# A message-passing layer on one core: two groups of edges in every stage of a step instead of one

## The chip, the core and the metric

The kernel runs on one core of one Trainium2 chip. A core has five engines with an instruction stream each: TensorE (PE: matrix products, with weight loads listed apart as PEld), VectorE (DVE), ScalarE (ACT), GpSimd (POOL) and SyncE (SP, which here only issues DMA transfers). They run side by side and wait for one another through semaphores. SBUF is the on-chip working memory, with 128 partitions; PSUM, to which PE writes, has eight banks of 512 fp32 values in each partition. The metric is the device time of one execution in microseconds (us), lower is better; the median of several runs is given.

## The reference

One graph layer with a residual and a layer norm, on N = 6250 nodes of D = 128 values and E = 100,000 edges sorted by destination, with a hidden width of H = 256. `layernorm` subtracts each row's mean and divides by the root of its variance plus 1e-5.

```python
msg_in = concatenate([x[src], x[dst]], axis=-1)          # E x 256
h = relu(msg_in @ Wm1 + bm1)                             # E x 256
h = relu(h @ Wm2 + bm2)                                  # E x 256
messages = h @ Wm3 + bm3                                 # E x 128
agg = segment_sum(messages, dst) / clip(count(dst), 1)   # N x 128
upd = relu(concatenate([x, agg]) @ Wn1 + bn1) @ Wn2 + bn2
out = layernorm(x + (x + upd))
```

## The kernel before

There are three stages.

**Tables (0 to about 84 us).** The first product is taken per node, not per edge: `atab` holds `x @ Wm1[:128]` in fp32 in DRAM, `btab` holds `x @ Wm1[128:]` as three bf16 terms. Index columns, destination windows and the products `x @ Wn1[:128]` (`x_part`, line 327, blocks of 512 nodes) are made beside them. Four blocks of `x_part` are kept for the edge loop: 9 and 12 for its first steps (`X_FIRST`), 10 and 11 for its end (`X_END`).

**Edge loop (about 84 to 1127 us).** It is written out, not a loop on the chip. The edges are cut into NG = 196 groups of GE = 512 (the last has two tiles of 128, the others four). A group passes through these stages:

- `fetch` (lines 431 and 437): POOL gathers the four tiles' rows of `atab` by source with four indirect DMAs; SP loads the rows of `btab` for each tile's window of 21 destinations with four DMAs. A ring of four `rows` buffers holds them. `destinations` (line 355), issued by ACT, brings the destination numbers of two groups at a time.
- `hot` (lines 452 and 455, DVE): two one-hot matrices of the destinations, `oht` for the first layer and `oh` for the sums.
- `first_layer`: PE turns the gathered rows (line 468) and adds the destinations' terms as products with `oht` (line 474), both in PE tiles of 64 rows, into `ph` (two PSUM banks); ACT applies bias and relu into `h1` (line 478).
- `second_layer`: PE multiplies by `w2` (line 487), two tiles into one bank at a time, in full 128x128 tiles; DVE writes `max(product, -b2)` into one of four buffers `h2` (line 489).
- `sums`: PE adds up the edges of each window, `oh.T @ h2` (line 495), in tiles of 32 columns, four windows side by side; ACT copies the bank (`part_of`, line 502).
- `add_up`: PE turns those sums (line 511, tiles of 64 rows), and DVE adds each window to the accumulator `acc` in SBUF at a place read from `tilei` (lines 516 and 519).

fp32 products of lines 487 and 495 appear as two records each in the trace.

The order of PE is the written one (`manual_schedule`) from the tables on. In each step i of the loop it is: sums of group g - 3, turning of group g - 4, first layer of group g = i - 2, second layer of group g - 1. So a whole step lies between the end of a group's second layer and its sums. DVE and ACT follow the written order up to step 6 (`turns.close()`); from there a scheduler orders them. The PSUM pools of the loop are `p1` (`ph`, one buffer of two banks), `p2` (`ph2`, two buffers of one bank), `pa` (`pg`, one bank) and `ptp` (`pt`, two banks). A last block under `manual_schedule` ends the loop with the three last groups and the blocks 10 and 11 of `x_part`.

**Nodes (about 1127 to 1202 us).** After a barrier (and a loop for windows that span too many nodes, empty here) the accumulated hidden sums are multiplied by `Wm3`, divided by the counts and taken through the node products and the layer norm.

Around the edge loop, `late_loads`, the filler of `dpad` and `double` (the table `x2tab`: twice x plus a bias, for the end) are spread over the steps.

Of the kernel before, what the change touches and what calls it, by code (L numbers as in the profile page):

```python
# [19 lines left out]
P = 128  # L20
# [7 lines left out]
def kernel(  # L28
# [109 lines left out]
    w1 = const.tile([P, 2, H], F32, name="w1")  # L138
# [12 lines left out]
    with tc.tile_pool(name="prep", bufs=1) as prep, tc.tile_pool(  # L151
# [3 lines left out]
    ) as pb:  # L155
        src_i = prep.tile([R, 2 * GE], I32, name="src_i", tag="src_i")
# [256 lines left out]
    with edge, tc.tile_pool(name="wk", bufs=2) as wk, tc.tile_pool(  # L413
        name="p1", bufs=1, space=PSUM
    ) as p1, tc.tile_pool(name="p2", bufs=2, space=PSUM) as p2, tc.tile_pool(
        name="pa", bufs=1, space=PSUM
    ) as pa, tc.tile_pool(name="pt", bufs=1, space=PSUM) as ptp:


        NH2 = 4  # L420
# [4 lines left out]
        def fetch(idx, nt, firsts):  # L425


            rows = ld.tile([P, (GT + 1) * H], F32, name="rows", bufs=4)
            ag = rows[:, :GT * H].rearrange("p (j h) -> p j h", j=GT)
            for j in range(GT):  # L430
                nc.gpsimd.indirect_dma_start(  # L431
                    out=ag[:, j, :], out_offset=None, in_=atab[:, :],
                    in_offset=bass.IndirectOffsetOnAxis(ap=idx[:, j:j + 1], axis=0))
            bw = rows[:, GT * H:].bitcast(BF16).rearrange("p (k h) -> p k h", k=2)
            for j, first in enumerate(firsts):
                terms = btab[ds(first, WB + 1)].rearrange("n c h -> (n c) h")
                nc.sync.dma_start(bw[j // 2 * NQ:(j // 2 + 1) * NQ, j % 2, :], terms[:NQ])
            return ag, bw
# [7 lines left out]
        def hot(db, pb_cols, dl, nt):  # L446


            n = nt * WN
            oht = wk.tile([P, 2, P], BF16, name="oht")  # L450
            for k in range(2):
                nc.vector.tensor_scalar(oht[:n, k, :], db[:n, k * P:(k + 1) * P], pb_cols[:n, k:k + 1], None,  # L452
                                        op0=ALU.is_equal)
            oh = wk.tile([P, GT, WN], F32, name="oh", bufs=4)
            nc.vector.tensor_tensor(oh[:, :nt, :], iota_n.to_broadcast([P, nt, WN]),  # L455
                                    dl.rearrange("p (j o) -> p j o", o=1).to_broadcast([P, nt, WN]),
                                    op=ALU.is_equal)
            return oht, oh
# [3 lines left out]
        def first_layer(ag, bw, oht, nt):  # L462
            nh = nt // 2
            ph = p1.tile([P, 2, HC, 2 * P], F32, name="ph")
            for c in range(HC):
                for u in range(GT):
                    for h in range(nh):
                        nc.tensor.matmul(ph[:, h, c, u * NQ:(u + 1) * NQ], ag[halves[h], u, c * P:(c + 1) * P],  # L468
                                         ident[halves[h], halves[h]], is_transpose=True,
                                         start=(c == 0 and u == 0), stop=False, skip_group_check=True)  # L470
            for c in range(HC):
                for k in range(2):
                    for h in range(nh):
                        nc.tensor.matmul(ph[:, h, c, k * P:(k + 1) * P], bw[halves[h], k, c * P:(c + 1) * P],  # L474
                                         oht[halves[h], k, :], start=False, stop=True, skip_group_check=True)
            h1 = wk.tile([P, HC, GE], F32, name="h1")
            for c in range(HC):
                nc.scalar.activation(h1[:, c, :nh * 2 * P].rearrange("p (h e) -> p h e", h=nh), ph[:, :nh, c, :],  # L478
                                     AF.Relu, bias=b1[:, c:c + 1])
            return h1  # L480

        def second_layer(h1, h2, nt):
            for j0 in range(0, nt, 2):
                ph2 = p2.tile([P, 2, H], F32, name="ph2")
                for a in range(2):
                    for c in range(HC):
                        nc.tensor.matmul(ph2[:, a, :], h1[:, c, (j0 + a) * P:(j0 + a + 1) * P],  # L487
                                         w2[:, c, :], start=(c == 0), stop=(c == HC - 1))
                nc.vector.tensor_tensor(h2[:, j0:j0 + 2, :H], ph2, nb2.to_broadcast([P, 2, H]), op=ALU.max)  # L489

        def sums(oh, h2, nt):

            pg = pa.tile([P, H + 1], F32, name="pg")
            for j in range(nt):
                nc.tensor.matmul(pg[j * WN:(j + 1) * WN, :], oh[:, j, :], h2[:, j, :],  # L495
                                 start=True, stop=True, skip_group_check=True)
            return pg

        def part_of(pg, nt):
            n = nt * WN  # L500
            part = wk.tile([P, H + 1], F32, name="part")
            nc.scalar.copy(part[:n, :], pg[:n, :])  # L502
            return part

        def add_up(part, firsts, nt):
            pt = ptp.tile([P, 2, 4 * P], F32, name="pt")[:, :, :(HC + 1) * NQ]
            pt = pt.rearrange("p h (c q) -> p h c q", q=NQ)
            for c in range(HC + 1):
                for h in range(nt // 2):
                    rows = part[halves[h], c * P:(c + 1) * P] if c < HC else part[halves[h], H:].to_broadcast([NQ, P])  # L510
                    nc.tensor.matmul(pt[:, h, c, :], rows, ident[halves[h], halves[h]], is_transpose=True,  # L511
                                     start=True, stop=True, skip_group_check=True)
            for j in reversed(range(nt)):
                window = acc[:, :, ds(firsts[j], WB)]
                k = j % 2 * WN
                nc.vector.tensor_add(window, window, pt[:, j // 2, :, k:k + WB])  # L516
# [28 lines left out]
        def bank_p1():  # L545
            return p1.tile([P, 2, HC, 2 * P], F32, name="ph")[:, 0]

        def bank_p2():
            return p2.tile([P, 2, H], F32, name="ph2")

        ahead, lag = 2, 3
        st, hots = {}, {}
        first = list(X_FIRST)
        for i in range(NG + ahead + 1):
            if i == 6:
                turns.close()
            if i == 16:
                late_loads()

                none = wk.tile([16, (NG * GE - E) // 16 + 1], I32, name="none", bufs=1)  # L560
                nc.vector.memset(none, NONE)
                nc.sync.dma_start(dpad[E - 16:].rearrange("(p e) -> p e", p=16), none)
                nc.sync.dma_start(dpad[:E].rearrange("(p e) -> p e", p=16), dst.rearrange("(p e) -> p e", p=16))
            for step, after in enumerate((20, 24, 27)):
                if i >= after and (i - after) % 8 == 0 and (i - after) // 8 < len(pieces):
                    double((i - after) // 8, step)
            if i < NG:
                nt = GT if i < NGF else LT
                firsts = load_bases(tilei[0:1, i * GT:(i + 1) * GT], nt, ENG.SP)
                if i == NGF:  # L570
                    dbs = last_destinations()
                elif i % 2 == 0:
                    dbs = early.pop(0) if early else destinations(i, min(2, NGF - i), dst_row)
                st[i] = dict(nt=nt, got=fetch(srcT[:, i, :], nt, firsts), db=dbs.pop(0))
            g = i - ahead
            if 0 <= g < NG:
                s = st[g]
                ag, bw = s.pop("got")

                def make_hot(g):  # L580
                    s = st[g]
                    hots[g], s["oh"] = hot(s.pop("db"), pbase[:, g, :], dloc[:, g, :s["nt"]], s["nt"])

                if g not in hots:
                    make_hot(g)
                oht = hots.pop(g)
            k = g - lag
            pg = sums(st[k]["oh"], st[k]["h2"], st[k]["nt"]) if 0 <= k < NG else None
            k = g - lag - 1
            if 0 <= k < NG:  # L590
                s = st.pop(k)
                if "firsts" not in s:
                    s["firsts"] = load_bases(tilei[0:1, k * GT:(k + 1) * GT], s["nt"], ENG.DVE)
                add_up(s["part"], s["firsts"], s["nt"])
            if 0 <= g < NG:
                s = st[g]
                s["h1"] = first_layer(ag, bw, oht, s["nt"])
            if pg is not None:
                st[g - lag]["part"] = part_of(pg, st[g - lag]["nt"])
# [220 lines left out]
```

## Time and profile before

| | |
|---|---|
| median of 3 runs | 1203.84 us (1203.38 to 1206.65) |
| the profiled execution | 1204.24 us, its span 1202.5 us |
| granted TensorE clock, mean | 0.996 |
| HBM | 160 GB/s over the span |

The window view gives the busy time of each engine in a stretch (us):

| stretch | PE | DVE | ACT | POOL | granted clock |
|---|---|---|---|---|---|
| 0 to 60 | 51.76 | 39.36 | 40.28 | 34.99 | 1.00 |
| 70 to 100 | 27.25 | 16.46 | 12.44 | 22.79 | 1.00 |
| 300 to 500 | 200.00 | 104.06 | 62.01 | 144.47 | 1.00 |
| 500 to 700 | 200.00 | 108.51 | 62.31 | 144.50 | 1.00 |
| 900 to 1100 | 200.00 | 109.57 | 62.30 | 142.38 | 1.00 |
| 1100 to 1130 | 27.27 | 13.74 | 8.26 | 0.20 | 0.97 |
| 1145 to 1202 | 49.29 | 45.85 | 34.42 | 9.09 | 0.95 |

How to read the lines that follow in the next section. In the page's groups, a line has the source line, the engine, the operation, what it writes and reads, the shape and the number of instructions; after the bar the busy time in us and the mean duration of one in ns; after the second bar the idle time of the engine just before them and what ended most of it. In a timeline, a line has the start in us from the span's start, the length, the engine and the merged group, with the idle time before it and its releaser in brackets. Ends of matmuls are modelled, and consecutive matmuls overlap, so the starts carry the information.

### The profile page before, as it was taken

What the parts mean: (1) busy time and instruction counts of PE and PEld (TensorE: products, weight loads), DVE (VectorE), ACT (ScalarE), POOL (GpSimd) and SP (SyncE); (2) the same over time, 40 slices, a digit from 0 to 9 for tenths busy, and PEclk for the clock granted to TensorE, in tenths of its full rate; (3) what the DMA queues carried; (4) which work ended last, traced back from release to release, by engine and by line L of the source; (5) the groups of instructions that cost most, each with busy time, mean ns of one, the idle gap of its engine ahead of it and who ended that gap; (6) DMA issues with size and microseconds to landing.
All of it is one profiled execution on the core that took longest, in us unless ns stands there. A gap on an engine that the chain in (4) does not pass through costs nothing. (4 is left out here: it accounts for less than half of the span.)

```text
span 1202.5 us, 32806 instructions
## 1 busy us (share of the span) xinstructions
PE 1180.1 (98%) x11196; PEld 896.9 (75%) x11197; DVE 675.7 (56%) x2077; ACT 419.2 (35%) x776; POOL 801.2 (67%) x862
## 2 busy tenths in 40 slices
PE   8999999999999999999999999999999999999997
PEld 6747777777777777777777777777777777777565
DVE  5764555555555455555555555555555555555587
ACT  5753332332332333233233323323323332332256
POOL 6567777777777777777777777777777777773120
PEclk9999999999999999999999999999999999999998
DMA  8886666676555555555555555555555555552243
GB/s 274 280 264 191 183 194 185 182 193 185 160 151 153 150 148 153 152 151 152 152 149 147 153 153 152 153 150 149 148 154 154 150 152 151 147 147 67 83 117 114
DMA packets 173733, 193.66 MB, mean 161 GB/s; under 512 B 30906, under 2 KB 145548, under 8 KB 173548
## 3 DMA queue, kind: packets, MB, share of 16 engines
q0 software_dynamic: 38160, 103.75, 31.5%
q1 hardware_dynamic: 106956, 61.93, 17.7%
q10 hardware_dynamic: 28448, 25.87, 7.3%
q8 instruction: 89, 1.46, 0.5%
q14 instruction: 80, 0.66, 0.2%
HBM read 168.92 MB, written 22.88 MB: 160 GB/s over the span
## 5 line engine op out<-in xcount | busy, mean ns | idle before, releaser
L431 POOL DMA_INDIRECT rows<-atab,srcT x784 | 749.0, 955 | 285.4 <-issue 181.0
L487 PE MATMUL ph<-w,h 128*128 128x256 f32 x3128 | 727.6, 386 | 0.1
L487 PEld LDWEIGHTS ph<-w,h 128*128 128x128 f32 x3128 | 579.0, 190 | 91.1 <-ACT x_sb L329 0.9
L489 DVE TENSOR_TENSOR h<-ph,nb 128x512 f32<-128x512 f32 x391 | 270.6, 693 | 388.7 <-PE ph L487 376.4
L478 ACT ACTIVATE h<-ph,b 128x512 f32<-128x512 f32 x392 | 247.3, 682 | 138.4 <-PE ph L474 133.1
L502 ACT COPY part<-pg 128x257 f32<-128x257 f32 x196 | 73.6, 376 | 575.5 <-PE pg L495 510.6
L516 DVE TENSOR_TENSOR acc<-acc,pt 128x63 f32 x782 | 172.0, 220 | 78.1 <-PE pt L511 20.5
L468 PE MATMUL ph<-ident,rows 64*128 64x64 f32 x3128 | 129.9, 223 | 1.3 <-ACT h L478 0.7
L495 PE MATMUL pg<-h,oh 128*32 128x257 f32 x1564 | 125.6, 392 | 0.0
L468 PEld LDWEIGHTS ph<-ident,rows 64*128 64x128 f32 x3128 | 113.1, 140 | 2.3 <-ACT h L478 0.9
L511 PEld LDWEIGHTS pt<-ident,part 64*128 64x128 f32 x1173 | 51.1, 137 | 81.5 <-issue 81.1
L452 DVE TENSOR_SCALAR oht<-db,pbase 128x128 bf16<-128x128 int32 x392 | 100.9, 289 | 0.1
L495 PEld LDWEIGHTS pg<-h,oh 128*32 128x32 f32 x1564 | 30.9, 108 | 65.8 <-issue 65.0
L511 PE MATMUL pt<-ident,part 64*128 64x64 f32 x1173 | 77.8, 239 | 0.1
L474 PE MATMUL ph<-oht,rows 64*128 64x128 bf16 x1564 | 76.1, 216 | 0.9 <-DMA rows<-btab 0.8
L701 POOL TENSOR_TENSOR agg<-total,rc 128x512 f32<-128x512 f32 (+2 forms) x15 | 16.0, 1069 | 69.5 <-DMA rcol<-acc 33.2
L455 DVE TENSOR_TENSOR oh<-iota_n,dloc 128x128 f32<-128x128 f32 x196 | 55.9, 285 | 0.0
L474 PEld LDWEIGHTS <-rows 64*128 64x128 bf16 x1564 | 53.2, 96 | 1.4 <-DMA rows<-btab 0.9
L235 PE MATMUL pbt<-w,xT 128*128 128x256 f32 x196 | 49.8, 398 | 3.9 <-DVE rest L255 1.2
L235 PEld LDWEIGHTS pbt<-w,xT 128*128 128x128 f32 x196 | 36.6, 198 | 13.4 <-DVE rest L255 2.9
L724 PEld LDWEIGHTS pot<-wu,u 128*128 128x128 f32 (+1 forms) x196 | 24.0, 191 | 5.1 <-issue 4.5
L696 PE MATMUL pmt<-acc,w 128*128 128x512 f32 (+2 forms) x60 | 24.8, 551 | 2.3 <-DVE rc L690 2.3
(111 smaller groups left out, 410.7 us busy)
## 6 DMA issues: line engine op xcount, KB each, us to landing
rows<-btab SPq DMA_DIRECT2D x782, 32.0 KB
db<-in_dst_dram ACTq DMA_DIRECT2D x194, 128.0 KB
rows<-atab,srcT POOLq DMA_INDIRECT x784
btab<-bt SPq DMA_DIRECT2D x24, 384.0 KB
atab<-bt SPq DMA_DIRECT2D x24, 256.0 KB
xd<-in_x_dram SPq DMA_DIRECT2D x12, 256.0 KB
x2tab<-xd SPq DMA_DIRECT2D x12, 256.0 KB
x_sb<-in_x_dram SPq DMA_DIRECT2D x5, 512.0 KB
```

The costliest lines, as they stand in the source:

```text
L235: nc.tensor.matmul(pbt[:, a, :], xT[:, (t0 + a) * P:(t0 + a + 1) * P], w1[:, k, :], start=True, stop=True)
L431: nc.gpsimd.indirect_dma_start(out=ag[:, j, :], out_offset=None, in_=atab[:, :], in_offset=bass.IndirectOffsetOnAxis(ap=idx[:, j:j + 1], a ...
L452: nc.vector.tensor_scalar(oht[:n, k, :], db[:n, k * P:(k + 1) * P], pb_cols[:n, k:k + 1], None, op0=ALU.is_equal)
L468: nc.tensor.matmul(ph[:, h, c, u * NQ:(u + 1) * NQ], ag[halves[h], u, c * P:(c + 1) * P], ident[halves[h], halves[h]], is_transpose=True, ...
L474: nc.tensor.matmul(ph[:, h, c, k * P:(k + 1) * P], bw[halves[h], k, c * P:(c + 1) * P], oht[halves[h], k, :], start=False, stop=True, skip ...
L478: nc.scalar.activation(h1[:, c, :nh * 2 * P].rearrange("p (h e) -> p h e", h=nh), ph[:, :nh, c, :], AF.Relu, bias=b1[:, c:c + 1])
L487: nc.tensor.matmul(ph2[:, a, :], h1[:, c, (j0 + a) * P:(j0 + a + 1) * P], w2[:, c, :], start=(c == 0), stop=(c == HC - 1))
L489: nc.vector.tensor_tensor(h2[:, j0:j0 + 2, :H], ph2, nb2.to_broadcast([P, 2, H]), op=ALU.max)
L495: nc.tensor.matmul(pg[j * WN:(j + 1) * WN, :], oh[:, j, :], h2[:, j, :], start=True, stop=True, skip_group_check=True)
L502: nc.scalar.copy(part[:n, :], pg[:n, :])
L511: nc.tensor.matmul(pt[:, h, c, :], rows, ident[halves[h], halves[h]], is_transpose=True, start=True, stop=True, skip_group_check=True)
L516: nc.vector.tensor_add(window, window, pt[:, j // 2, :, k:k + WB])
```

## The change

The step of the loop now takes two groups (98 pairs, `NP`).

- `fetch`, `hot`, `first_layer`, `sums` and `part_of` get a list of groups. `rows` has two buffers of two groups, `ph` four banks (one buffer), `oht` and `h1` hold two groups; there are two `h2` buffers, one for each group of a pair, and six `oh`.
- The other four banks are the pool `p2`, two tiles of two banks (`banks()`), used in turn by `sums`, by the turning (`turned`, split off from `add_up`) and by the second layer of each group. `second_layer` writes a group's four products into one such tile; its max is one instruction (128x1024) for the first group of a pair and two of 128x512 for the second (`cuts`).
- A pair's step: sums of pair p - 2, turning of pair p - 3, then DVE's first addition, the copy of the sums, the other additions, the `x2tab` step, the comparisons for pair p + 1; PE's first layer of pair p; second layer of pair p - 1. The sums of a pair come directly after its second layer.
- The copy of the sums is one DVE instruction for both groups (128x514) instead of an ACT copy for each.
- DVE and ACT follow the written order to the end of the loop.
- `w1` moves to a pool that ends with the tables. The steps at which `late_loads` and `double` stand are halved. At the end, three products of `x_part` stand ahead of the last sums and one behind them.

```diff
-        def second_layer(h1, h2, nt):
-            for j0 in range(0, nt, 2):
-                ph2 = p2.tile([P, 2, H], F32, name="ph2")
-                for a in range(2):
-                    for c in range(HC):
-                        nc.tensor.matmul(ph2[:, a, :], h1[:, c, (j0 + a) * P:(j0 + a + 1) * P],
-                                         w2[:, c, :], start=(c == 0), stop=(c == HC - 1))
-                nc.vector.tensor_tensor(h2[:, j0:j0 + 2, :H], ph2, nb2.to_broadcast([P, 2, H]), op=ALU.max)
+        def banks():
+            return p2.tile([P, 2, 2 * H], F32, name="banks")
...
+        def second_layer(h1, h2, nt, cuts):
+            ph2 = banks().rearrange("p b (t h) -> p (b t) h", t=2)
+            for j in range(nt):
+                for c in range(HC):
+                    nc.tensor.matmul(ph2[:, j, :], h1[:, c, j * P:(j + 1) * P],
+                                     w2[:, c, :], start=(c == 0), stop=(c == HC - 1))
+            step = nt // cuts
+            for j in range(0, nt, step):
+                nc.vector.tensor_tensor(h2[:, j:j + step, :H], ph2[:, j:j + step],
+                                        nb2.to_broadcast([P, step, H]), op=ALU.max)
...
+        def sums(groups):
+            pg = banks()
+            for i, (oh, h2, nt) in enumerate(groups):
+                for j in range(nt):
+                    nc.tensor.matmul(pg[j * WN:(j + 1) * WN, i, :H + 1], oh[:, j, :], h2[:, j, :],
+                                     start=True, stop=True, skip_group_check=True)
+            return pg
...
-            nc.scalar.copy(part[:n, :], pg[:n, :])
+                nc.vector.tensor_copy(part[:, :n], pg[:, :n, :H + 1])
...
+        def turned(part, nts):
+            pt = banks()[:, :, :2 * (HC + 1) * NQ].rearrange("p h (g c q) -> p h g c q", g=2, q=NQ)
...
+        for i in range(NP + 4):
...
+            if i < NP:
+                dbs = early.pop(0) if early else destinations(2 * i, min(2, NGF - 2 * i), dst_row)
...
+                got = fetch([(srcT[:, 2 * i + k, :], firsts) for k, firsts in enumerate(bases(i, ENG.SP))])
...
+            p = i - 1
...
+            k = p - 3
+            firsts = bases(k, ENG.DVE) if k >= 0 else None
+            pg = pt = None
+            if 0 <= p - 2 < NP - 1:
+                pg = summed(p - 2)
+            if 0 <= k:
+                pt = turned(st[k]["part"], st[k]["nts"])
+            if p - 2 == NP - 1:
+                whole(x for x, _ in zip(rest, range(2)))
+                pg = summed(p - 2)
+                whole(rest)
+            adds = add_up(pt, firsts, st[k]["nts"]) if pt is not None else iter(())
+            next(adds, None)
+            if pg is not None:
+                st[p - 2]["part"] = part_of(pg, st[p - 2]["nts"])
+            whole(adds)
...
+            for step, after in enumerate((10, 12, 14)):
+                if i >= after and (i - after) % 4 == 0 and (i - after) // 4 < len(pieces):
+                    double((i - after) // 4, step)
+            if p + 1 < NP:
+                make_hot(p + 1)
+            if p < NP:
+                s = st[p]
+                s["h1"] = first_layer(s.pop("got"), s.pop("ohts"), s["nts"])
+            if p < 2:
+                whole(x_part(X_FIRST[p], bank, (nc.scalar, nc.vector)))
+            if 0 <= p - 1 < NP:
+                s = st[p - 1]
+                for k, nt in enumerate(s["nts"]):
+                    second_layer(s["h1"][:, k], h2s[k], nt, 1 + k)
```

`summed(p)` calls `sums` on both groups of pair p; `bases(p, engine)` reads the windows' first nodes of both groups into registers of that engine; `make_hot(p)` calls `hot` on both.

## Prediction, before the result was known

> **What bounds the kernel now.** I read the page first, then the timeline of one stretch of the edge loop, first TensorE alone, then all engines. The chain of waits is no help here: it reaches back only to the barrier before the node stage (5% of the span on PE).
>
> ```profile
> PE 1180.1 (98%) x11196; PEld 896.9 (75%) x11197; DVE 675.7 (56%) x2077; ACT 419.2 (35%) x776; POOL 801.2 (67%) x862
> ...
> PEclk9999999999999999999999999999999999999998
> ...
> L431 POOL DMA_INDIRECT rows<-atab,srcT x784 | 749.0, 955 | 285.4 <-issue 181.0
> L487 PE MATMUL ph<-w,h 128*128 128x256 f32 x3128 | 727.6, 386 | 0.1
> ```
>
> PE is busy 98% of the span at nearly the full granted clock, and its largest group idles 0.1 us in all. So TensorE's own stream is the bound, and what counts is how long one turn of it takes:
>
> ```profile
> 504.60 0.64 PE L495 MATMUL pg<-h,oh 128*32 128x257 f32 x8
> 505.17 0.40 PE L511 MATMUL pt<-ident,part 64*128 64x64 f32 x6
> 505.41 0.66 PE L468 MATMUL ph<-ident,rows 64*128 64x64 f32 x16
> 505.91 0.39 PE L474 MATMUL ph<-oht,rows 64*128 64x128 bf16 x8
> 506.22 3.72 PE L487 MATMUL ph<-w,h 128*128 128x256 f32 x16
> 509.87 0.64 PE L495 MATMUL pg<-h,oh 128*32 128x257 f32 x8
> ```
>
> Start to start a group costs 0.57 (sums) + 0.24 (turning) + 0.50 + 0.31 (first layer) + 3.65 (second layer) = 5.27 us, 10.55 a pair. The second number of a line is a modelled busy time that overlaps the next line; starts are what to add. The other engines around one such turn:
>
> ```profile
> 502.98 0.69 DVE L489 TENSOR_TENSOR h<-ph,nb 128x512 f32<-128x512 f32 x1 [0.95 <-PE ph L487]
> ...
> 504.59 0.16 PEld L495 LDWEIGHTS pg<-h,oh 128*32 128x32 f32 x8 [0.33 <-issue]
> 504.60 0.64 PE L495 MATMUL pg<-h,oh 128*32 128x257 f32 x8
> 504.70 0.69 DVE L489 TENSOR_TENSOR h<-ph,nb 128x512 f32<-128x512 f32 x1 [1.03 <-PE ph L487]
> ```
>
> Here is the point: the last max of a second layer (504.70 to 505.39) runs beside the sums of the group before it (504.60), whose own maxes ended a step ago. PE never waits for the last max. The changed kernel sums the groups whose second layer has just ended.
>
> **Gain: fewer changes of tile shape.** In the single records of this stretch, L487 records start 216 ns apart inside a run. The last L487 to the first L495 takes 309 (93 too many); the last L495 to L511 310 (94, against the same 216); the first pair of turnings takes 117 instead of 61 (about 55); the last L474 to L487 takes 146 instead of 56 (90), and the second L487 comes 319 after the first (103). Together 0.43 us, once a group now, once a pair afterwards. All other records stay: a pair without waits is 2 x 5.27 - 0.43 = 10.12 us.
>
> **Cost: the wait at the head.** Call L the start of the pair's last L487-type record.
> - L + 0.41: DVE can start the max (504.29 to 504.70 in the records).
> - In the changed program as built, the second group's max is cut in two, but the first cut carries one wait for PE and the second none, and PE signals once, on the last of the group's eight matmuls. In the old program each L489 has a wait of its own. So the first cut does not start halfway through the group; both follow the last matmul. The first runs L + 0.41 to 1.10 (692 ns, the L489 row). A second such instruction behind one without a wait starts 0.60 after it (the pair L711 at 1143.24 and 1143.84), so it ends at L + 0.41 + 0.60 + 0.69 = 1.70.
> - PE starts 52 ns after a DVE instruction that it waited for (64.468 to 64.520), so the third and fourth sums of the second group start at L + 1.76.
> - The first group's sums (from L + 0.31, two rounds of 241 ns, done dispatching by 0.79) and the second group's first two (from 1.16) are ready earlier. PE starts a group's four 32-column tiles together, so what is left is two rounds and a change of shape: 1.76 + 0.24 + 0.01 + 0.31 = L + 2.32 for the first turning.
> - Without a wait it would be L + 0.31 + 3 x 0.24 + 0.02 + 0.31 = 1.36. The stall is **0.96 us a pair**.
>
> Behind the waiting sums on PE stand, in program order, the turnings, the next first layer and the next second layer: nothing can pass them. A pair becomes 10.12 + 0.96 = **11.08 us** against 10.55.
>
> Here two rules of the Trainium skill speak. "TensorE: Matmul & The Clock Gate", The cost: per-tile semaphore tail, recommends one increment, on the last matmul, which saves some 26 ns for each one left out (fitted to packed small tiles); no row here shows it. And "PSUM — Partial Sum Buffer", PSUM bank collisions raise a hardware error, asks for a guard by bank (and quadrant), no coarser: the two cuts read different banks of the two-bank tile, so the first could start halfway. By these two a signal in the middle would cost 0.03 us (an estimate from the former) and make the stall that of one cut: sums at L + 1.10 + 0.05 = 1.16 instead of 1.76, so 0.36 and a pair of 10.47. By the built order it is 0.96. I take the built order: no speed can start an instruction before its wait.
>
> **The rest of the step.**
> - DVE, in one written order now, has eight adds (0.25 each from 505.93 on), the copy of the sums (128x514, not in the trace; between 0.69 as L489's 512 and 0.75 as two L502 rows of 376; 0.70 taken), four L452 (0.20 apart), two L455 (0.28), and maxes of some 1.23 + 0.60 + 0.69: about 7 of 11.08 us. The adds start near L + 2.9, the copy ends near L + 3.9, before the second layer needs its banks at L + 2.32 + 0.42 + 1.00 + 0.54 = 4.28; the comparisons end near L + 7.1, the next max is due at 11.08 - 3.46 + 0.41 = 8.0. Hidden. Uncovered, the copy would cost what it is late.
> - ACT loses two L502 (0.38 each). Nobody waits for ACT there: nothing.
> - Destinations' DMAs stand behind four relus on ACT (issued near L + 7, two of 0.6) and are needed at the next L + 5.7: hidden by 8 us.
> - POOL needs 1.258 us a gather (503.81 to 505.07), 8 a pair: 10.06. The buffers still hold four groups but come free by pairs; a pair's gathers have two steps less a first layer, 22.2 - 1.6, for 10.06 and a landing of some 2. Hidden at 11.08. At 10.12 it would be nearly a second bound.
> - SP's eight btab issues take 0.65 each: 5.2 of 11.08. The x2tab steps, late loads and w1's other pool add no instruction.
>
> **Filling and draining.** Before, group 2's second layer starts at 100.17. Now the first layer of pair 0 waits for eight btab rows (SP issues from 80.9 every 0.65, landing 2.5 later: 88.2), the next for ACT's four relus and its own eight rows (93.5); the second layer of pair 0 comes behind it, at 94.8 to 101.9, its sums with their wait end in time for the next first layer at 104.0, and pair 1's second layer starts at 105.6: +5.4. At the end, from the start of group 192's second layer (1102.1) the old kernel needs 24.5 us to ACT's last L329 (1126.57). The new one has last record at +6.8, first turning +9.1, the short pair's second layer +9.7 to 15.1, turnings, three of the four L327 products one behind another through one free buffer (1.8 each), sums and copies, the last product, turnings and six adds: 27.6, so +3.1.
>
> **Sum.** 95 pairs x (11.08 - 10.55) = 50.4, + 5.4 + 3.1 = 58.9. The profiled execution took 1204.24 (span 1202.5), so 1263.1; the median shown is 0.4 lower, so **1263 us**, +4.9%.
>
> **Rivals.**
> - *The first cut starts halfway*, as its bank would allow. For it: the cut is in the code. Against: the built order has no wait to do it with. Stall 0.36: 1204.2 + 95 x (10.47 - 10.55) + 8.5 less 0.6 of the fill = 1204.5, no change. This is the mechanism that ends on the other side: the price per pair is stall minus 0.43, plus 8.5 / 95 = 0.09 for the ends, so below a stall of 0.34 the kernel is faster; fully covered it is 1204.2 - 41 + 8 = 1171. 7%.
> - *The stall is right and DVE is also late*: in one written order a late destination or the 0.69 us of an x2tab step (L540) pushes the maxes, and PE behind them. For it: DVE no longer picks what is ready. Against: about 1 us of slack by the sum above. At 0.3 us a pair more: 1292. 7%.
> - *The clock falls* because PE now idles once a step. Against: PE's gap is under 1 us in 11; the profile's early slices with gaps (0 to 60 us: PE busy 51.8) have the clock at 1.00. 3%.
>
> The likeliest case has 83%, with its own range 1250 to 1276 (0.1 us a pair in the wait or the switches is 9.5 us, the ends 4). To leave out no more than 2 in 10, 1245 to 1280. A measurement tells 0.3%, 3.6 us, from no change: faster 4%, within 3%, slower 93%.
>
> **What would show it.** PE's step 11.1 us instead of 10.55; two 128x512 maxes back to back after the pair's last matmul, PE idle before the second group's sums with DVE as releaser, near 0.9 us each and 80 to 90 in all; POOL idle before its gathers up by about 0.5 a pair. Wrong if the first cut starts some 1.7 us before the last matmul, or if a step is below 10.6.

## The result, and the profile after

The changed kernel takes **1265.01 us** (median of 4 runs, 1263.87 to 1265.66) against 1203.83 us of the kernel before beside it: 1.050 times as long, 95% interval 1.048 to 1.052. The forecast was 1263. The profiled execution has a span of 1263.3 us, +60.8. Of several runs of one kernel, those more than 1.5% above its fastest are left out of a ratio; in the table further down this concerns two of the six runs of e2_one_max and one of the four of e3_lag, whose times there are medians of all their runs.

From the page of the changed kernel (busy times, the granted clock, and three of its groups):

```profile
PE 1212.7 (96%) x11196; PEld 913.6 (72%) x11197; DVE 709.7 (56%) x2077; ACT 335.1 (27%) x580; POOL 802.0 (63%) x862
...
PEclk9989999999999999999999999999999999999899
...
L437 POOL DMA_INDIRECT rows<-atab,srcT x784 | 749.3, 956 | 334.0 <-issue 198.0
...
L511 PEld LDWEIGHTS banks<-h,oh 128*32 128x32 f32 x1564 | 43.6, 108 | 145.5 <-DVE h L503 82.4
...
L519 DVE COPY part<-banks 128x514 f32<-128x514 f32 x97 | 66.5, 685 | 0.7 <-issue 0.7
```

The same 11196 matmul records, a granted clock of 0.992 against 0.996 (1.00 in both from 300 to 700 us, in the middle of the loop), and still 96% busy: the busy share alone hides the loss. What tells it is the sums' weight loads (L511), which now stand idle 145.5 us in all, 82.4 of it until a max of VectorE. In the kernel before, the same group read:

```profile
L495 PEld LDWEIGHTS pg<-h,oh 128*32 128x32 f32 x1564 | 30.9, 108 | 65.8 <-issue 65.0
```

One turn of the loop, from the timeline of TensorE alone (start, length, and in brackets the idle time before):

```profile
504.52 7.17 PE L499 MATMUL banks<-w,h 128*128 128x256 f32 x32
511.63 0.64 PE L511 MATMUL banks<-h,oh 128*32 128x257 f32 x8
512.48 1.22 PE L511 MATMUL banks<-h,oh 128*32 128x257 f32 x8 [0.21 <-issue]
513.63 0.58 PE L533 MATMUL banks<-ident,part 64*128 64x64 f32 x12
514.05 1.16 PE L478 MATMUL ph<-ident,rows 64*128 64x64 f32 x32
515.05 0.61 PE L485 MATMUL ph<-oht,rows 64*128 64x128 bf16 x16
515.59 1.78 PE L499 MATMUL banks<-w,h 128*128 128x256 f32 x7
```

From L499 to L499 it is 11.06 us; the kernel before needs 10.55 for two groups. Two groups' sums last from 511.63 to 513.63, 2.00 us, where two separate ones took 1.14. The timeline of all engines shows why:

```profile
511.73 1.29 DVE L503 TENSOR_TENSOR h<-banks,nb 128x512 f32<-128x512 f32 x2 [2.23 <-PE banks L499]
...
513.08 0.14 PEld L511 LDWEIGHTS banks<-h,oh 128*32 128x32 f32 x4 [0.45 <-DVE h L503]
513.63 0.44 PEld L533 LDWEIGHTS banks<-ident,part 64*128 64x128 f32 x12 [0.41 <-issue]
```

Both maxes of the second group (merged into one line, x2) start after the last matmul, although VectorE had been idle for 2.23 us; 0.06 us after the second one ends, the last four records of the sums (the third and fourth tile of that group, two records each) start.

### The profile page after: what moved, and what is told of

Its sections match the earlier page's. It is cut to its first block, busy times and chain, and to the rows that moved or that the text cites. A ratio compares the mean times of both kernels' runs of the same rounds, so it can differ in the third digit from the quotient of the medians.

```text
span 1263.3 us, 31888 instructions
## 1 busy us (share of the span) xinstructions
PE 1212.7 (96%) x11196; PEld 913.6 (72%) x11197; DVE 709.7 (56%) x2077; ACT 335.1 (27%) x580; POOL 802.0 (63%) x862
## 5 line engine op out<-in xcount | busy, mean ns | idle before, releaser
L437 POOL DMA_INDIRECT rows<-atab,srcT x784 | 749.3, 956 | 334.0 <-issue 198.0
L499 PE MATMUL banks<-w,h 128*128 128x256 f32 x3128 | 701.3, 382 | 1.4 <-DVE acc L542 1.0
L499 PEld LDWEIGHTS banks<-w,h 128*128 128x128 f32 x3128 | 586.2, 190 | 87.5 <-issue 1.1
L491 ACT ACTIVATE h<-ph,b 128x512 f32<-128x512 f32 x392 | 236.6, 685 | 840.6 <-PE ph L485 829.0
L503 DVE TENSOR_TENSOR h<-banks,nb 128x512 f32<-128x512 f32 (+1 forms) x294 | 245.6, 864 | 354.2 <-PE banks L499 314.0
L542 DVE TENSOR_TENSOR acc<-acc,banks 128x63 f32 x782 | 171.5, 219 | 140.4 <-PE banks L533 114.0
L511 PE MATMUL banks<-h,oh 128*32 128x257 f32 x1564 | 181.8, 392 | 21.6 <-DVE h L503 12.0
L511 PEld LDWEIGHTS banks<-h,oh 128*32 128x32 f32 x1564 | 43.6, 108 | 145.5 <-DVE h L503 82.4
L478 PE MATMUL ph<-ident,rows 64*128 64x64 f32 x3128 | 114.4, 223 | 0.6 <-issue 0.6
L533 PEld LDWEIGHTS banks<-ident,part 64*128 64x128 f32 x1173 | 43.2, 136 | 41.6 <-issue 39.7
L519 DVE COPY part<-banks 128x514 f32<-128x514 f32 x97 | 66.5, 685 | 0.7 <-issue 0.7
L485 PE MATMUL ph<-oht,rows 64*128 64x128 bf16 x1564 | 60.9, 216 | 3.4 <-DMA rows<-btab 3.4
L533 PE MATMUL banks<-ident,part 64*128 64x64 f32 x1173 | 56.6, 229 | 0.8 <-ACTq L650 0.8
L485 PEld LDWEIGHTS <-rows 64*128 64x128 bf16 x1564 | 48.9, 95 | 4.0 <-DMA rows<-btab 3.9
```

Source lines behind the costliest of these rows:

```text
L437: nc.gpsimd.indirect_dma_start(out=ag[:, j, :], out_offset=None, in_=atab[:, :], in_offset=bass.IndirectOffsetOnAxis(ap=idx[:, j:j + 1], a ...
L478: nc.tensor.matmul(ph[:, i, h, c, u * NQ:(u + 1) * NQ], ag[halves[h], u, c * P:(c + 1) * P], ident[halves[h], halves[h]], is_transpose=Tru ...
L485: nc.tensor.matmul(ph[:, i, h, c, k * P:(k + 1) * P], bw[halves[h], k, c * P:(c + 1) * P], ohts[halves[h], i, k, :], start=False, stop=Tru ...
L491: nc.scalar.activation(h1[:, i, c, :nh * 2 * P].rearrange("p (h e) -> p h e", h=nh), ph[:, i, :nh, c, :], AF.Relu, bias=b1[:, c:c + 1])
L499: nc.tensor.matmul(ph2[:, j, :], h1[:, c, j * P:(j + 1) * P], w2[:, c, :], start=(c == 0), stop=(c == HC - 1))
L503: nc.vector.tensor_tensor(h2[:, j:j + step, :H], ph2[:, j:j + step], nb2.to_broadcast([P, step, H]), op=ALU.max)
```

## The experiments

The theory: a step is TensorE's own stream, 10.1 us, plus a stall of about 1 us, and the stall is the wait for two maxes that begin only after the pair's last matmul, because the wait belongs to the two-bank tile and not to its halves. The rivals: VectorE is late for other reasons; TensorE gained nothing from fewer changes of tile shape.

Twelve runs came in four series, each on another chip and with the kernel before beside it:

| run | time (us) | kernel before beside it | ratio, 95% interval |
|---|---|---|---|
| e1_banks | 1701.10 | 1401.43 | 1.212 [1.207, 1.217] |
| e2_one_max | 1741.10 | 1401.43 | 1.235 [1.232, 1.239] |
| e3_lag | 1728.03 | 1401.43 | 1.231 [1.226, 1.235] |
| e4_both | 1665.68 | 1401.43 | 1.189 [1.184, 1.193] |
| e4_again | 1179.03 | 1204.35 | 0.979 [0.977, 0.980] |
| e1_again | 1213.84 | 1204.72 | 1.008 [1.006, 1.009] |
| e3_again | 1222.52 | 1204.72 | 1.014 [1.013, 1.016] |
| e2_again | 1259.83 | 1204.72 | 1.046 [1.044, 1.047] |
| e5_split | 1243.12 | 1204.72 | 1.032 [1.031, 1.034] |
| e6_terms | 2096.17 | 1421.40 | 1.476 [1.473, 1.479] |
| e7_best | 1726.76 | 1421.40 | 1.214 [1.210, 1.217] |
| e8_banks_fill | 1788.33 | 1421.40 | 1.262 [1.255, 1.271] |

In the first series (the first four rows) and the last (the last three) the kernel before itself took 1401 and 1421 us instead of 1204, so no total time of these two series is read as a property of an edit. The four kernels of the first series were run again beside a kernel before of 1204 us; the three of the last were not.

The traces of these two series still hold something usable. Nearly all their steps take 12 to 21 us while the gathers run, but the first step (from sums to sums) that begins after the last gather takes what it takes elsewhere:

| kernel | that step in the first or last series | the same step beside a kernel before of 1204 us |
|---|---|---|
| e1_banks, e1_again | 10.467 us | 10.463 us |
| e2_one_max, e2_again | 11.015 | 11.011 |
| e3_lag, e3_again | 10.570 | 10.570 |
| e4_both, e4_again | 10.056 | 10.057 |
| e6_terms | 10.360 | not run |
| e7_best | 10.062 | not run |
| e8_banks_fill | 10.464 | not run |

It is one step of one execution each, with no gathers beside it. Below, "the step" without more is the mean over the middle of the loop in a series with a kernel before of 1204 us; it is 10.547 us for two groups in the kernel before and 11.064 in the changed one.

### The second group's maxes read one-bank tiles (e1_banks, e1_again)

```diff
+        def one():
+            return p3.tile([P, 2 * H], F32, name="one")
...
+            if cuts == 1:
+                whole2 = banks().rearrange("p b (t h) -> p (b t) h", t=2)
+                parts = [(0, nt, whole2)]
+            else:
+                parts = [(j, 2, one().rearrange("p (t h) -> p t h", t=2)) for j in range(0, nt, 2)]
...
-            pt = banks()[:, :, :2 * (HC + 1) * NQ].rearrange("p h (g c q) -> p h g c q", g=2, q=NQ)
+            pt = [one()[:, :2 * (HC + 1) * NQ].rearrange("p (g c q) -> p g c q", g=2, q=NQ) for _ in range(2)]
```

`p2` then has one two-bank buffer, `p3` two of one bank.

> The second group's two maxes read two separate one-bank tiles, so the first may start after four of the eight matmuls. Theory (the stall of 0.95 us a pair is the wait for both maxes after the pair's last matmul, because the wait belongs to the two-bank tile): the first max starts more than 1 us before the last matmul, only the second is left behind it, the second group's third and fourth sums start 1.16 instead of 1.76 us after the last matmul, the step falls from 11.06 to 10.46 us, and 95 pairs give 1265 - 57 = 1208 us. Rival A (VectorE is late for other reasons, such as its written order): the step stays near 11.0 and the time near 1260. Rival B (the second max alone hides beside the first group's sums): step 10.12, 1175 us.

> The kernel of e1_banks once more, on a chip where the kernel before takes 1204 us. Theory (the wait belongs to the two-bank tile): the first of the two maxes starts 1.7 us before the pair's last matmul, the second one stays behind it, the step falls from 11.06 to 10.46 us and the time to 1208 us. Rival A (VectorE is late for other reasons): step near 11.0, 1260 us. Rival B (the second max alone hides beside the first group's sums): step 10.06, 1173 us.

The step is 10.467 us, the forecast 10.46 to 10.47. VectorE's timeline of e1_again, a step whose last matmul (L509) starts at 515.89:

```profile
512.86 1.22 DVE L511 TENSOR_TENSOR h<-banks,nb 128x1024 f32<-128x1024 f32 x1 [1.42 <-PE banks L509]
514.58 0.69 DVE L511 TENSOR_TENSOR h<-one,nb 128x512 f32<-128x512 f32 x1 [0.50 <-PE one L509]
516.31 0.69 DVE L511 TENSOR_TENSOR h<-one,nb 128x512 f32<-128x512 f32 x1 [1.03 <-PE one L509]
```

The first cut now starts 1.3 us before the last matmul (1.7 was expected: it starts 0.42 after the eighth of the group's sixteen records), and only one is left behind it. Nothing in VectorE's order was changed, so rival A falls; the remaining 0.41 us a pair (10.467 less the 10.06 that follows below) is against rival B. The time came out 5.8 us over the 1208. The first pair's second layer starts at 99.83 us instead of 95.52, the second pair's at 111.36 instead of 106.22. In the timeline of TensorE, the node products of the first two steps (L327) now use the single two-bank tile one behind another:

```profile
88.23 2.08 PE L327 MATMUL banks<-xT,wu 128*128 128x512 f32 x2
91.44 2.08 PE L327 MATMUL banks<-xT,wu 128*128 128x512 f32 x2 [1.14 <-DMA rows<-atab,srcT]
...
98.93 0.47 PE L327 MATMUL banks<-xT,wu 128*128 128x106 f32 x2 [2.36 <-ACT x_sb L329]
```

ACT copies the bank out (L329) behind its four relus, at 90.69 to 91.39; the third product starts 0.05 later, so it is most likely this that it waited for, and not the bracket's DMA (in the second pair the bracket names the copy). With the start 5.1 us later, 1265.0 - 95 x 0.597 + 5.1 = 1213.4 us; 1213.84 was measured.

### One max for the second group (e2_one_max, e2_again)

```diff
-                    second_layer(s["h1"][:, k], h2s[k], nt, 1 + k)
+                    second_layer(s["h1"][:, k], h2s[k], nt, 1)
```

> The second group's max is one instruction of 128x1024 as the first group's is. Theory (the cut buys nothing, since both parts wait for the last matmul and PE starts a group's four sums together): the max ends 1.63 instead of 1.70 us after the last matmul, the step falls by 0.07 us, 95 pairs give -6 us: 1259 us. Rival (the cut lets the first two sums of the second group run ahead): the step grows by 0.2 to 0.6 us, 1284 to 1320 us.

> The kernel of e2_one_max once more, on a chip where the kernel before takes 1204 us. Theory: the one max ends 1.63 instead of 1.70 us after the last matmul, the step is 10.99 instead of 11.06 us, and the time 1259 us (1.046 of the kernel before, against 1.050). Rival (the cut lets the first two sums of the second group run ahead): step 11.2 to 11.6, 1284 to 1320 us.

1259.83 us, step 11.015. VectorE's timeline of e2_again, a step whose last matmul starts at 508.76:

```profile
505.73 1.22 DVE L503 TENSOR_TENSOR h<-banks,nb 128x1024 f32<-128x1024 f32 x1 [1.43 <-PE banks L499]
509.18 1.22 DVE L503 TENSOR_TENSOR h<-banks,nb 128x1024 f32<-128x1024 f32 x1 [2.23 <-PE banks L499]
```

The one max starts 0.42 us after the last matmul, where the first of the two cuts started. So the cut, in a shared tile, is worth less than nothing: it costs 0.05 us a pair (11.064 against 11.015; 0.07 expected).

### The second group summed one step later (e3_lag, e3_again)

```diff
+        def unit(q):
+            return [g for g in (2 * q - 1, 2 * q) if 0 <= g < NG]
...
-        def summed(p):
-            s = st[p]
-            return sums([(s["ohs"][i], h2s[i], s["nts"][i]) for i in range(2)])
+        def summed(q):
+            return sums([(ohs.pop(g), h2_of(g), NTS[g]) for g in unit(q)])
```

There are three `h2` buffers and seven `oh`; `part` and `xd` go down to one buffer for their room, and the `x2tab` steps stand closer together.

> The second group of each pair is summed one step later (together with the next pair's first group), so no sum waits for a max that has just begun; the banks are as in the change. Theory: PE's sums run at once, but the turning behind them writes the two-bank tile that the second group's maxes still read until 1.70 us after the last matmul; it starts at 1.76 instead of 2.32 (1.36 without any wait), so the stall falls from 0.95 to 0.40, the step to 10.51 us and the time to 1265 - 53 + 2 for the longer end = 1214 us. Rival A (the sums' wait is the whole stall): step 10.12, 1177 us. Rival B (VectorE or the transfers set the step): 1240 us or more.

> The kernel of e3_lag once more, on a chip where the kernel before takes 1204 us. Theory: the sums no longer wait, the turning behind them still waits for the two-bank tile that the second group's maxes read until 1.70 us after the last matmul; turning at 1.76 (2.32 in the change), step 10.50 us, 1214 us. Rival A (the sums' wait is the whole stall): step 10.06, 1178 us. Rival B (VectorE or the transfers set the step): 1240 us or more.

1222.52 us, step 10.600. The timeline of e3_again around its last matmul at 513.85:

```profile
514.16 1.07 PE L511 MATMUL banks<-h,oh 128*32 128x257 f32 x16
514.27 1.29 DVE L503 TENSOR_TENSOR h<-banks,nb 128x512 f32<-128x512 f32 x2 [2.23 <-PE banks L499]
...
515.70 0.58 PE L533 MATMUL banks<-ident,part 64*128 64x64 f32 x12 [0.47 <-DVE h L503]
```

The sixteen records of the sums run in one piece, and the wait has moved to the turning, which needs the two-bank tile that the maxes still read: a second, hidden price of the same tile, as the theory said. The step is 0.10 us longer than expected (10.600 against 10.50). The second max ends at 515.555 and the turning starts 146 ns later; in the changed kernel the sums start 55 ns after it. The turning is also a change of tile shape, and the difference, 91 ns, is near the 94 of such a change: it would then be paid behind the wait and not during it. No run separates the shape from the other differences between a turning and a sum.

### Both (e4_both, e4_again)

The two diffs above together.

> Both edits together: the second group summed one step later, and its maxes and the turning in one-bank tiles. Theory: both waits are gone, the step is PE's own stream with one set of tile-shape changes a pair, 10.12 us (GpSimd's gathers need 10.06), and the time 1265 - 90 + 2 = 1177 us, 2.2% under the kernel before. Rival A (fewer changes of tile shape save nothing): step 10.5, 1214 us. Rival B (gathers become the bound, with waits of their own): step 10.3 to 10.4, 1195 to 1205 us, with GpSimd idle under 1% of the loop.

> The kernel of e4_both once more: in its first series the kernel before took 1401 us beside it instead of 1204, and the maxes started up to 5.7 us after the last matmul instead of 0.4. If that belonged to the chip of that series (its semaphores from TensorE late), a chip on which the kernel before takes 1204 gives the theory's 1177 us with a step of 10.12 us. If it belongs to the edit, the time stays above 1400 us whatever the kernel before takes.

**1179.03 us**, 2.1% under the kernel before (ratio 0.979, 0.977 to 0.980) and 6.8% under the changed kernel. The step is 10.060 us. The timeline of e4_again, one head of a step:

```profile
508.95 0.69 DVE L511 TENSOR_TENSOR h<-one,nb 128x512 f32<-128x512 f32 x1 [0.50 <-PE one L509]
...
510.57 1.07 PE L519 MATMUL banks<-h,oh 128*32 128x257 f32 x16
510.67 0.69 DVE L511 TENSOR_TENSOR h<-one,nb 128x512 f32<-128x512 f32 x1 [1.03 <-PE one L509]
511.57 0.44 PEld L541 LDWEIGHTS one<-ident,part 64*128 64x128 f32 x12 [0.41 <-DVE h L511]
511.57 0.58 PE L541 MATMUL one<-ident,part 64*128 64x64 f32 x12
```

and its window view (us in the stretch: PE, PEld, DVE, ACT, POOL, then the granted clock, the DMA share and GB/s):

```profile
500.00:700.00 200.00, 200.00 (x2156) 164.21 (x2155) 125.15 (x364) 48.49 (x80) 151.45 (x159) 1.00 0.61 168
```

Maxes and sums lie side by side again. In the single records, sums to first turning takes 1.005 us here and 2.009 in the changed kernel; the other four pieces of a step (turning, two parts of the first layer, second layer) agree within 0.002. So the whole stall of the change lies at that head and was 11.064 - 10.060 = 1.00 us a pair, and the saving from stages that come once a pair is real: 10.547 - 10.060 = 0.49 us. GpSimd's gathers also follow each other without a wait, one every 1.258 us, 10.06 for eight: it has become a second bound. The kernel gives some of it back outside: 5.1 us at the start as in e1_again, 4.3 at the end (one more short step).

### Two more changes of shape (e5_split)

On e4_both: `first_layer` becomes a generator that yields after each group, and the second group's half stands between the second layers.

```diff
+                both = first_layer(s.pop("got"), s.pop("ohts"), s["nts"])
+                s["h1"] = next(both)
...
                 for k, nt in enumerate(s["nts"]):
+                    if k:
+                        whole(both)
```

> On e4_both: the second group's part of the first layer stands between the two groups' second layers, so that a pair has five changes of tile shape instead of three; no record is added. Theory (a change of shape costs TensorE time, as between the old kernel's stages): the 64-row to 128-row change costs 0.19 us (90 at the change and 103 at the second record in the old trace), the other way 0.09 to 0.15, the step goes from 10.06 to 10.34-10.40 us and the time from 1179 to 1206-1211 us. Rival A (the saved 0.43 us a pair came from something else, such as fewer waits): step 10.06 to 10.1, 1179 to 1183 us. Rival B (the later first layer brings a wait, for ScalarE's relu or the gathers): over 1225 us, with such a releaser in the trace.

1243.12 us, step 10.738: more than any of the expectations but B, and the timeline of e5_split shows a wait:

```profile
507.30 0.69 DVE L525 COPY part<-banks 128x514 f32<-128x514 f32 x1
...
507.45 0.39 PE L491 MATMUL ph<-oht,rows 64*128 64x128 bf16 x8
...
508.13 3.69 PE L507 MATMUL banks<-w,h 128*128 128x256 f32 x16 [0.29 <-DVE acc L548]
```

The releaser in brackets is not the right one: what frees the bank is the copy of the sums, which ends at 507.984, 146 ns ahead of the product. With half the first layer in front of it, the second layer is due at 507.76 and starts at 508.13. In the single records this wait is worth 0.34 us net. The two added changes are there too: 94 and 54 ns from L507 to L485, 90 and 105 from L491 to L507, together 0.34. The sum is 10.06 + 0.34 + 0.34 = 10.74, as measured. So rival A falls, since the added changes are seen in the records. Rival B came true in part: a wait, but for VectorE's copy and not for ScalarE's relu or the gathers. The split of the loss is read here from a kernel that has both. A kernel without the wait is e6_terms (only the products of the second group with its one-hot matrices between the second layers):

> As e5_split, but only the eight products with the second group's one-hot matrices stand between the two second layers; both groups' turnings stay together, so the copy of the sums is done before the first second layer is due (508.04 against 508.26 in the times of e5_split). Five changes of tile shape a pair, no wait. Theory (each pair of changes costs what the single records of e5_split show, 0.34 us, and the rest of that kernel's loss was the wait for the copy): step 10.06 + 0.34 = 10.40 us, time 1179 + 95 x 0.34 = 1211 us. Rival A (changes of shape are nearly free and the wait was all): step 10.1, 1183 us. Rival B (something else delays in both): step 10.7, 1243 us.

It fell into the last series (2096 us beside 1421), so its time says nothing. Its one step behind the last gather does, from the timeline of TensorE (that pair's second group has only two tiles, so four products stand between):

```profile
1979.10 1.07 PE L518 MATMUL banks<-h,oh 128*32 128x257 f32 x16
...
1981.83 3.72 PE L508 MATMUL banks<-w,h 128*128 128x256 f32 x16
1985.48 0.39 PE L492 MATMUL ph<-oht,rows 64*128 64x128 bf16 x4
1985.81 3.72 PE L508 MATMUL one<-w,h 128*128 128x256 f32 x16
1989.46 0.86 PE L518 MATMUL banks<-h,oh 128*32 128x257 f32 x12
```

Nothing waits, and the step is 10.360 us: 0.30 more than the 10.06 of e4_both, where the theory had 0.34, rival A next to nothing and rival B 0.6. So two added changes of shape cost 0.30 us by themselves, and most of the rest of e5_split's loss, 0.38, is its wait (0.34 by its records). It rests on one step.

### Repairing the start (e7_best, e8_banks_fill)

```diff
-                whole(x_part(X_FIRST[p], bank, (nc.scalar, nc.vector)))
+                whole(x_part(X_FIRST[p], lambda: one().rearrange("p (t h) -> p t h", t=2), (nc.scalar, nc.vector)))
```

> On e4_both: the node products at the loop's first two steps (L327) get the two one-bank tiles instead of the single two-bank tile, which they used one behind another. Theory: the first second layer starts near 95.9 instead of 100.4 us, the step stays 10.06, time 1179 - 4.5 = 1174.5 us, 2.5% under the kernel before. Rival (the btab rows of the first pairs set the start anyway): 1178 to 1179 us.

> On e1_banks: the same edit to the first node products. Theory (e1_banks came out 5.8 us over its sum because its start lost 4.3 us to the single two-bank tile): 1213.8 - 4.3 = 1209.5 us with the step unchanged at 10.47. Rival (the loss is at the end, through the same tile): 1213 us.

Same series, so their times say nothing. Behind the last gather their steps are 10.062 and 10.464 us, unchanged as expected. The trace of e7_best shows that the four products at the start then run in one piece:

```profile
96.04 3.78 PE L327 MATMUL one<-xT,wu 128*128 128x512 f32 x4
```

against twice 2.08 with 1.14 between them. Whether 4.5 us (4.3 for e8_banks_fill) come of it was not measured.

## Why the prediction was right, point by point

- **What bounds**: TensorE's stream, at the same clock in the loop (1.00). Confirmed by every run beside a kernel before of 1204 us: the time follows TensorE's step, and the rival of a falling clock did not happen.
- **Gain, 0.43 us a pair, 10.12 without waits**: 0.49 and 10.060 in e4_again. The sum took the four rounds of the sums (four records each) to start 241 ns after one another, as in the two rounds of the kernel before; in one piece they start 241, 217 and 216 ns after one another, so the first turning comes 1.31 us after the last matmul and not 1.36.
- **Stall, 0.96**: 1.00 by the difference to e4_again. The single steps hold: second max to L + 1.70 (measured 513.02, L = 511.32), sums at 1.76 (513.08), first turning at 2.32 (513.635, which is 2.32). So the end of the wait was right; the 1.36 without a wait, from which the stall was counted, was 0.05 too long, and the gain too small by as much. In the step the two errors cancel. VectorE was not late besides (the first cut starts at L + 0.42), so the rival of a late VectorE did not happen.
- **Step 11.08**: 11.064. The sign "TensorE idle before the second group's sums, 80 to 90 us in all" stands on the weight loads (82.4 until a max); the matmul row of L511 itself shows 21.6, since its modelled ends cover most of the wait.
- **The copy, 0.70 and hidden**: 685 ns, hidden. e5_split shows how thin that cover is: with half a first layer in front, the same copy costs 0.34 us.
- **GpSimd idle up by 0.5 a pair**: its gathers' idle time went from 285.4 to 334.0 us, 0.50 for each of 98 pairs. That it would be nearly a second bound without the stall is what e4_again found.
- **Fill +5.4, drain +3.1**: the second pair's second layer starts at 106.22 (105.6 predicted, +6.05 in place of +5.4), and the node stage at 1187.44 instead of 1128.16, +59.3, which leaves 59.3 - 95 x 0.517 - 6.05 = 4.1 for the drain. The sum, 49.1 + 6.05 + 4.1 against 50.4 + 5.4 + 3.1, has errors of both signs. The stage of the nodes, which the sum put at nothing, is 1.5 us longer (75.8 against 74.3; in the other runs it is 74.6 to 76.0, and why is open), and together this makes the 60.8. That the forecast of 1263 came within 2 us of 1265 is in part luck: steps 1.3 too many, ends and nodes 3.2 too few.
- **Rival "the first cut starts halfway"**: it did not happen in the change, and e1_again makes it happen. Its step was put at 10.47 and is 10.467, its time at 1204.5, and the experiment, with a start 5 us worse, took 1213.84. The guard by bank that the Trainium skill asks for ("PSUM — Partial Sum Buffer", PSUM bank collisions raise a hardware error) is the one that pays here: 0.60 us a pair (11.064 to 10.467). The page gives it as a rule of safety, against a guard by address; that it should be "no coarser" is the prediction's addition. The saving of one increment, some 26 ns in "TensorE: Matmul & The Clock Gate", The cost: per-tile semaphore tail, was not measured by itself in any run.
- **"Fully covered", named at 1171 within that rival**: e4_again, 1179.03; its step is 0.06 us below the 10.12 and its two ends are 9.4 us longer than the change's.

## What to carry to other kernels

When a consumer is moved directly behind its producer, write down the last matmul, the wait that the reader between them carries, and the time to that reader's end: here 1.0 us a pair against a gain of 0.49. An instruction cut in two started early here only when each half had a tile, and so a wait, of its own (e1_again against the change). One step of distance for the late half (a third `h2` buffer) and tiles of one bank turned +5.0% into -2.1%, but only together: either alone left a stall of 0.41 or 0.54 us, because the next wait stood right behind the one taken away.

## What was not expected

**The same kernel and another kernel before.** e4_both and e4_again are one kernel: 1665.68 us where the kernel before took 1401.43, 1179.03 where it took 1204.35. So the penalty there is not a common factor: 1.16 for the old kernel, 1.41 for this one. In e4_both's profile the mean granted clock is 0.867 (0.983 in e4_again), but the kernel before had 0.99 in that series and was still 197 us longer, so the clock alone doesn't explain it. VectorE's timeline of e4_both, where the last matmul record (L509) is at 818.93:

```profile
820.06 0.69 DVE L511 TENSOR_TENSOR h<-one,nb 128x512 f32<-128x512 f32 x1 [2.95 <-PE one L509]
822.94 0.69 DVE L511 TENSOR_TENSOR h<-one,nb 128x512 f32<-128x512 f32 x1 [2.19 <-remote]
```

The second max starts 4.0 us after that record, where 0.42 is usual, and the turning waits for it. The window view of e4_both, before and in the step that begins after the last gather (which ends at 1540.3), shows when this ends:

```profile
1400.00:1553.70 153.70, 121.55 (x1101) 99.28 (x1100) 63.24 (x183) 24.23 (x40) 74.04 (x78) 0.89 0.37 101
1553.70:1563.70 10.00, 10.00 (x97) 8.23 (x96) 4.89 (x12) 2.00 (x4) 0.00 (x0) 1.00 0.00 0
```

From then on the steps are those of e4_again (10.056 and 10.057 us), and the stage of the nodes takes 75.2 us against 76.0. So the loss lies in the stretch in which gathers and the other loads of the loop run. Which of these transfers delays the waits between the engines on these two chips, and why the kernels with pairs lose more than the kernel before, was not found out; of the kernel before there is no trace from those series. What it shows is that the ratio of two kernels measured in such a series says little about the ratio elsewhere: 1.189 there, 0.979 here.

**A first product after a wait is later where the tile shape changes**: 146 ns from VectorE's end to a turning (e3_again; 145 to 147 in 97 pairs) or to the first product of a second layer (147 in e5_split), 55 ns where the shape stays (the changed kernel's sums). That the shape is the cause is argued from this, not tested.
